# The linear score term of a graph attention layer, computed as four column groups over 128 tokens each and spread over the partitions by two transfers

## The chip, the cores and the metric

The kernel runs on one core of a Trainium2 chip. The metric is the device time of one execution in microseconds, as the median of several runs. All data are float32.

## The reference, cut to what matters

Four graph layers run over 64 graphs of 256 nodes with 128 features. Each layer takes a layer norm and a ReLU of x, applies a graph network with the shared matrix adj, and adds the result to x. The first layer is a gated network of five steps, the second a Chebyshev filter, the third a normalised convolution. The change is in the fourth, an attention layer whose pairwise scores are by far the largest piece of work:

```python
W1, W2 = (W[:, :F], W[:, F:])            # W is adj, 256 x 256; F = 128
s1 = jnp.einsum('bkf,ef->bke', x, W1)    # e runs over 256
s2 = jnp.einsum('bkf,ef->bke', x, W2)
pre = s1[:, :, None, :] + s2[:, None, :, :] + b_lin
h = jnp.where(pre >= 0, pre, ALPHA * pre)      # ALPHA = 0.2
e = jnp.einsum('bije,e->bij', h, a) + bias     # bias is adj
attn = jax.nn.softmax(e, axis=2)
out = jax.nn.sigmoid(jnp.einsum('bij,bjf->bif', attn, x))
```

The leaky rectifier is split into a clamped part, whose weighted sum over e needs one value for every (i, j, e), and a linear part. Of the linear part, what depends on i alone drops out of the softmax over j; what remains is ALPHA times the sum over e of a_e times s2_je. That is one number for each token j of each graph, the same for every row i. The kernel calls it `lin`.

## The kernel before

**Tiling.** The 64 graphs go in 32 pairs. A pair's activations are 128 x 512 tiles: features on the partitions, 2 x 256 tokens along the free dimension. A pair has two parts.

**The front** (`front(p)`) runs layers 0 to 2 of pair p and prepares layer 3: it makes `hT`, the normalised input by feature, and from it, each by one call of `project` and one eviction by ScalarE (ACT), the tiles `s2a`/`s2c` (first half of e), `lin`, `s2n`, `s1b` and `s1a`. `project` is four matmuls of 32 output columns each, which write four 32-partition strips of one PSUM bank over 512 tokens. For `lin` the stationary tile is `g2`, whose 128 columns are all the same vector, so that the bank holds the one wanted row 128 times, once on every partition. `copied` evicts it to SBUF with a 128 x 512 copy.

**The scores.** For each pair there are 128 score tiles (`NSLOT` = 32 x 64 positions, each with two halves of e, so 4096 in all). A tile `rl` is 128 x 2048: the clamped values of four rows i. It is made on VectorE (DVE) by one instruction (L652), on ACT by eight (L665), or on GpSimd (POOL) by eight (L672). TensorE (PE) reduces a tile over e with four matmuls of 32 columns over 512 (L709). Who makes a tile is not fixed: the kernel's planner decides it.

**The tail** (`tail(p, ic, ...)`) ends a block of 64 tiles: DVE adds adj to the summed scores (L558), POOL adds `lin` (L562), DVE takes the maximum (L566), ACT exponentiates (L571), PE transposes and multiplies with `h3`, ACT and POOL finish the output (L597 to L602), and the SP queue stores it (L604). There are 64 tails. `lin` is read nowhere else.

**What sets the order.** When the program is built, a list scheduler (the loop at the end of the kernel function) steps through time. Every front and tail is a generator that yields the engine of its next step and the time from which that step can run; `ran` advances an engine's planned clock by a hand-written cost, for example `PROJECT` = 0.86 for a `project` and `COPY` = 0.48 for an eviction. Whenever an engine is free by plan, the scheduler gives it a tail's step, else a front's step, else a score tile, and `in_order` then fixes the order of the engine's instructions for good. PE scores the tile that has been ready longest. At most 8, 3 and 2 tiles may be held unscored by DVE, ACT and POOL (`MOST`), and 13 buffers hold tiles. The costs therefore decide how the 4096 tiles are divided among DVE, ACT and POOL. A front may run ahead of its due time by a few steps only (`chain_ready`). Three PSUM banks are handed out by `take()` and come back through `spare`.

The SP queue issues the loads of x (`load_x(p + 1)`, when front p begins) and the stores of the tails, in the order in which the scheduler emitted them.

Of the kernel before, what the change touches and what calls it, by code (L numbers as in the profile page):

```python
# [8 lines left out]
F32 = mybir.dt.float32  # L9
# [5 lines left out]
P = 128  # L15
# [5 lines left out]
PE, DVE, ACT, POOL = ENGINES = (mybir.EngineType.PE, mybir.EngineType.DVE, mybir.EngineType.Activation, mybir.EngineType.Pool)  # L21
# [4 lines left out]
def kernel(  # L26
# [50 lines left out]
    nc = tc.nc  # L77
# [7 lines left out]
    work = ctx.enter_context(tc.tile_pool(name="work", bufs=2))  # L85
    relu_pool = ctx.enter_context(tc.tile_pool(name="relu", bufs=3))
    psum = ctx.enter_context(tc.tile_pool(name="psum", bufs=1, space=PSUM))
    banks = [psum.tile([P, NB * N], F32, name=f"bank{k}") for k in range(8)]
    s2v = banks[:2]
    s2p = banks[2].rearrange("p (b n) -> p b n", b=NB)  # L90
# [1 line left out]


    clock = dict.fromkeys((PE, DVE, ACT, POOL), 0.0)
    SEEN = {PE: 0.25, DVE: 0.14, ACT: 0.18, POOL: 0.13}
    behind = [0.0]

    def ran(engine, us, *after):
        start = max(clock[engine], 0.0, *after)
        if engine == ACT:  # L100
            behind[0] = max(0.0, behind[0] - (start - clock[ACT])) + 0.024 * us
        clock[engine] = start + us
        return clock[engine] + SEEN[engine] + (behind[0] if engine == ACT else 0.0)

    spare = [[b, 0.0] for b in banks[5:]]

    def take():

        spare.sort(key=lambda b: b[1])
        return spare.pop(0)  # L110

    def by_feature(b):
        return b.rearrange("p (b n) -> p b n", b=NB)
# [11 lines left out]
    def in_order():  # L125

        traced = nc.cur_bb.bb.instructions
        for ins in traced[done[0]:]:
            if ins.engine not in ENGINES:
                continue  # L130
            if ins.engine in last:
                tc.add_manual_dep(ins, last[ins.engine],
                                  mybir.DependencyInfo(mybir.DependencyClass.NoSync, mybir.DependencyReason.DATA),
                                  reason="program order")
            last[ins.engine] = ins.name
        done[0] = len(traced)
# [115 lines left out]
    g2 = const.tile([P, P], F32, name="g2")  # L252
# [8 lines left out]
    def side_by_side(o, w, t, start=True, stop=True):  # L261

        for g in range(0, P, 32):
            nc.tensor.matmul(o[g:g + 32], w[:, g:g + 32], t, start=start, stop=stop, skip_group_check=True)  # L264

    def flat(t):
        return t.rearrange("p b n -> p (b n)")

    def project(pp, w, t, start=True, stop=True):

        side_by_side(pp, w, flat(t), start, stop)
# [30 lines left out]
    def feat(name, **kw):  # L302
        return work.tile([P, NB, N], F32, name=name, **kw)
# [10 lines left out]
    PROJECT, MIX, TURN, PRODUCT, PRODUCTS = 0.86, 1.74, 0.69, 0.88, 2.64  # L314
    COPY, BIASED, TANH, ELEMENTS = 0.48, 0.58, 0.57, 0.61

    def norm(src, since, h):

        stats = work.tile([P, NB * NC, 6], F32, name="stats")
        mv = work.tile([P, NB * NC, 2], F32, name="mv")  # L320
        s, h = rows_of(src), rows_of(h)
        yield DVE, since
        for k in range(NB * NC):
            nc.vector.bn_stats(stats[:, k, :], s[:, k, :])  # L324
        for k in range(NB * NC):
            nc.vector.bn_aggr(mv[:, k, :], stats[:, k, :])  # L326
        nc.vector.tensor_scalar(mv[:, :, 0], mv[:, :, 0], -1.0, None, op0=OP.mult)  # L327
        t = ran(DVE, 1.12, since)
        yield POOL, t
        inverse_root(mv[:, :, 1], OP.add, LN_EPS)  # L330
        nc.gpsimd.tensor_mul(mv[:, :, 0], mv[:, :, 0], mv[:, :, 1])  # L331
        t = ran(POOL, 1.4, t)
        yield ACT, t
        for k in range(NB * NC):
            nc.scalar.activation(h[:, k, :], s[:, k, :], AF.Relu, bias=mv[:, k, 0:1], scale=mv[:, k, 1:2])  # L335
        return ran(ACT, 1.54, t)

    def copied(name, bank, t):

        c = feat(name, **(SHORT if name not in KEPT else KEPT[name]))  # L340
        nc.scalar.copy(c, by_feature(bank[0]))  # L341
        t = ran(ACT, COPY, t)
        spare.append([bank[0], t])
        return c, t

    KEPT = {"hT": dict(bufs=4), "hT3": {}, "s2n": {}, "lin": {}}

    READY = {}

    def front(p):  # L350
# [8 lines left out]
        t = yield from norm(x0, 0.0, h)  # L359
        yield PE, t, 1  # L360
        b = take()
        to_feature(b[0], h)
        t_h = t
        t = ran(PE, TURN, t, b[1])
        yield ACT, t
        hT, t_hT = copied("hT", b, t)
        for step in range(STEPS):
            yield PE, t_h, 1
            b = take()
            mix_nodes(b[0], h, adj_t)  # L370
            t = ran(PE, MIX, t_h, b[1])
# [6 lines left out]
            t = ran(PE, 2 * PROJECT, t_m, t_hT, pr[1])  # L378
# [3 lines left out]
            t = ran(ACT, TANH, t, r[1])  # L382
# [11 lines left out]
            t = ran(PE, 2 * PROJECT, t_rh, pv[1])  # L394
# [5 lines left out]
            t = ran(ACT, TANH, t)  # L400
# [4 lines left out]
            t = ran(DVE, ELEMENTS, t)  # L405
# [7 lines left out]
            hT = hT_new  # L413
            t_hT = ran(DVE, ELEMENTS)
            spare.append([pr[0], t_hT])
            yield PE, t_hT, 1
            b = take()
            to_token(b[0], hT)
            t = ran(PE, TURN, t_hT, b[1])
# [9 lines left out]
        t = ran(DVE, ELEMENTS, t)  # L429
# [6 lines left out]
        b = take()  # L436
        mix_nodes(b[0], h, adj_n)
        t = ran(PE, MIX, t_h, b[1])
# [3 lines left out]
        b = take()  # L442
        to_feature(b[0], h)
        t = ran(PE, TURN, t_h, b[1])
        yield ACT, t
        hT, t = copied("hT", b, t)
        yield PE, t_h, 1
        b = take()
        mix_nodes(b[0], h, adj_2)
        t = ran(PE, MIX, t_h, b[1])  # L450
        yield ACT, t
        c2T, t = copied("c2T", b, t)
# [3 lines left out]
        t = ran(PE, PRODUCTS, t, po[1])  # L456
# [7 lines left out]
        t = ran(DVE, ELEMENTS)  # L464
# [4 lines left out]
        t = yield from norm(x2, t, h)  # L469
        yield PE, t, 1  # L470
        b = take()
        mix_nodes(b[0], h, adj_ti)
        t = ran(PE, MIX, t, b[1])
        yield ACT, t
        yT, t = copied("yT", b, t)
# [3 lines left out]
        t = ran(PE, PRODUCT, t, po[1])  # L479
# [3 lines left out]
        t = ran(DVE, ELEMENTS, t)  # L483
# [3 lines left out]
        t = ran(ACT, COPY, t)  # L487
# [3 lines left out]
        t = ran(DVE, ELEMENTS, t)  # L491
        yield POOL, t
        inverse_root(rn, OP.max, NORM_EPS * NORM_EPS)
        t = ran(POOL, 1.25, t)
# [3 lines left out]
        for k in range(NB * NC):  # L498
            nc.vector.scalar_tensor_tensor(rows_of(x3)[:, k], pt[:, k], rn[:, k:k + 1], rows_of(x2)[:, k],
                                           op0=OP.mult, op1=OP.add)  # L500
        t = ran(DVE, 1.04, t)
# [4 lines left out]
        t = yield from norm(x3, t, h3)  # L506
        yield PE, t, 1
        b = take()
        to_feature(b[0], h3)
        t = ran(PE, TURN, t, b[1])  # L510
        yield ACT, t
        hT, t_hT = copied("hT3", b, t)
# [7 lines left out]
        t_s2c = t_s2a = ran(ACT, COPY, t_s2a)  # L520
        yield PE, t_hT, 1
        b = take()
        project(b[0], g2, hT)
        t = ran(PE, PROJECT, t_hT, b[1])
        yield ACT, t
        lin, t_lin = copied("lin", b, t)
        yield PE, t_hT, 1
        b = take()
        project(b[0], w2n[:, P:2 * P], hT)
        t = ran(PE, PROJECT, t_hT, b[1])  # L530
        yield ACT, t
        s2n, t_2 = copied("s2n", b, t)
        yield PE, t_hT, 1
        b = take()
        project(b[0], adj_t[:, 0, P:2 * P], hT)
        t = ran(PE, PROJECT, t_hT, b[1])
# [6 lines left out]
        b = take()  # L543
        project(b[0], adj_t[:, 0, 0:P], hT)
        t = ran(PE, PROJECT, t_hT, b[1])
# [6 lines left out]
                        since=(max(t_n, t_s2a, t_s2c), max(t_b, t_2)))  # L552
# [75 lines left out]
    def tile_ready(e):  # L628

        if e in begun:  # L630
            return 0.0
        n = following[half(e)]
        if n >= NSLOT or n // SLOTS not in READY or held[e] == MOST[e] or not tiles:
            return None
        return max(READY[n // SLOTS]["since"][half(e)], min(t[1] for t in tiles))
# [90 lines left out]
    def begin_front():  # L726
        p = begun_fronts[0]
        load_x(p + 1)
        begin(p, front(p))
        begun_fronts[0] += 1  # L730

    def chain_ready(key, e):

        engine, since, bank, gate = (*CHAINS[key][1], 0, None)[:4] if len(CHAINS[key][1]) < 4 else CHAINS[key][1]
        if engine != e or bank and not spare or gate and not gate():
            return None
        if not isinstance(key, tuple) and key > 0 and spare:

            due = STEPS_OF_FRONT * (scored[0] / (2 * SLOTS) - (key - 2)) / SPREAD
            if CHAINS[key][2] > due + AHEAD:  # L740
                return None
        return max(since, min(b[1] for b in spare)) if bank else since
# [7 lines left out]

    in_order()
    now = dict.fromkeys(clock, 0.0)
    for e in clock:
        clock[e] = 0.0
    while scored[0] < 2 * NSLOT or CHAINS:
# [4 lines left out]
        for key in CHAINS:  # L760
            since = chain_ready(key, e)
# [6 lines left out]
        else:  # L768
            since = tile_ready(e)
# [47 lines left out]
```

## Time and profile before

| | us |
|---|---|
| median of 3 runs | 5358.55 (5358.25 to 5358.73) |
| the profiled execution's own time | 5354.23 |
| its span | 5352.4 |
| PE busy, of the span | 5241.4 (98%) |
| DVE busy | 5221.7 (98%) |
| ACT busy | 5121.4 (96%) |
| POOL busy | 5160.9 (96%) |
| PE weight loads (PEld), overlapping PE | 1861.5 (35%) |

| `lin` and its neighbours | count | busy us | mean ns |
|---|---|---|---|
| PE matmuls `bank<-hT,g`, 128 x 512 | 256 | 34.2 | 607 |
| ACT copy of `lin`, 128 x 512 | 32 | 28.8 | 900 |
| POOL addition of `lin`, 128 x 512 | 64 | 84.3 | 1317 |

Busy time of a group is the union of its instructions' spans, and a mean is the length of one instruction's own span; instructions of one engine overlap in the profile, so what an instruction costs its engine is read from the distance between starts. The profile shows two records for every float32 matmul of the program: a `project` of four matmuls appears as eight. In the groups, L264 is the line of `side_by_side`, which serves all projections, and L341 that of `copied`.

### The profile page before, as it was taken

The page shows a single profiled execution, that of the slowest core. Times are in us where ns is not written, and L with a number is a line of the kernel's source. Part 1 is how long each engine was busy: PE and PEld are TensorE (multiplying, and loading weights), DVE is VectorE, ACT ScalarE, POOL GpSimd, SP SyncE. Part 2 cuts the span into 40 slices and gives each one's busy share as a digit, 9 for nine tenths or more (in the row PEclk, how much of TensorE's full clock was granted, in tenths as well). Part 3 has the DMA queues.
Part 4 walks back from the last instruction along what each step waited for, and adds up shares of the span by engine and source line. Part 5 has one row for each costly group of instructions (what it writes and reads, how often), then busy time and mean ns, then how long its engine had stood idle before and what let it go on. Part 6 is the DMA issues. An engine that isn't in the chain of part 4 may idle for free.

```text
span 5352.4 us, 138977 instructions
## 1 busy us (share of the span) xinstructions
PE 5241.4 (98%) x56085; PEld 1861.5 (35%) x56085; DVE 5221.7 (98%) x4322; ACT 5121.4 (96%) x13465; POOL 5160.9 (96%) x5974
## 2 busy tenths in 40 slices
PE   6999999999999999999999999999999999999998
PEld 2333333333333333333333333333333333333332
DVE  3999999999999999999999999999999999999998
ACT  3999999999999999999999999999999999999999
POOL 0999999999999999999999999999999999999999
PEclk9999999999999999999999999999999999999999
DMA  0000000000000000000000000000000000000000
GB/s 17 5 5 6 6 3 6 6 5 6 5 4 6 5 6 5 3 6 6 5 5 4 4 6 5 6 6 3 6 5 6 6 5 3 6 5 4 4 2 4
DMA packets 38839, 26.99 MB, mean 5 GB/s; under 512 B 3504, under 2 KB 38192, under 8 KB 38192
## 3 DMA queue, kind: packets, MB, share of 16 engines
q1 hardware_dynamic: 35088, 17.05, 1.1%
q8 instruction: 438, 7.18, 0.6%
q14 instruction: 209, 1.71, 0.1%
q10 hardware_dynamic: 3104, 1.05, 0.1%
HBM read 9.70 MB, written 8.39 MB: 3 GB/s over the span
## 4 chain that ended last, share of the span: by engine, by line
PE 49%; DVE 34%; POOL 9%; ACT 5%; issue 4%; DMA 0%; POOLq 0%; SPq 0%; DVEq 0%; ACTq 0%
PE bank L709 32%; DVE rl L652 28%; PE bank L264 15%; POOL rl L672 7%; ACT rl L665 3%; PE bank L292 1%; DVE d L404 1%; DVE stats L324 1%; DVE bank L408 1%; DVE hT L412 1%; DVE rh L385 1%; PE bank L285 1%; POOL sc L562 0%; DVE mv L327 0%; POOL mv L259 0%
## 5 line engine op out<-in xcount | busy, mean ns | idle before, releaser
L672 POOL TENSOR_SCALAR rl<-s2n,s1b 128x256 f32<-128x256 f32 x5328 | 4786.0, 940 | 9.7 <-ACT s1b L539 9.7
L652 DVE TENSOR_TENSOR rl<-s1a,bank 128x2048 f32<-128x2048 f32 x2015 | 4484.6, 2276 | 12.1 <-ACT s1a L548 12.1
L665 ACT ACTIVATE rl<-bank,s1b 128x256 f32<-128x256 f32 x11056 | 4392.2, 839 | 1.3
L709 PE MATMUL bank<-rl,win_n 128*32 128x512 f32 x21448 | 2654.8, 593 | 33.9 <-DVE rl L652 31.9
L709 PE MATMUL bank<-rl,win 128*32 128x512 f32 x11320 | 1487.2, 593 | 0.0
L709 PEld LDWEIGHTS bank<-rl,win_n 128*32 128x32 f32 x21448 | 678.9, 110 | 1496.4 <-issue 1214.0
L709 PEld LDWEIGHTS bank<-rl,win 128*32 128x32 f32 x11320 | 365.9, 110 | 754.4 <-issue 630.2
L264 PE MATMUL bank<-adj_t,h 128*32 128x256 f32 x5120 | 310.0, 381 | 3.8 <-ACT h L423 3.8
L264 PEld LDWEIGHTS bank<-adj_t,h 128*32 128x32 f32 x5120 | 166.6, 110 | 174.3 <-issue 58.6
L335 ACT ACTIVATE h<-x,mv 128x128 f32<-128x128 f32 x384 | 172.1, 634 | 43.3 <-POOL mv L331 42.9
L264 PE MATMUL bank<-hT,u3t 128*32 128x512 f32 x1280 | 169.5, 593 | 0.0
L264 PE MATMUL bank<-mT,w4t 128*32 128x512 f32 x1280 | 169.4, 592 | 0.0
L264 PE MATMUL bank<-mT,w 128*32 128x512 f32 x1280 | 166.8, 593 | 0.5 <-ACT bank L381 0.5
L264 PE MATMUL bank<-mT,w5t 128*32 128x512 f32 x1280 | 166.7, 592 | 0.4 <-DVE rh L385 0.4
L264 PE MATMUL bank<-rh,u5t 128*32 128x512 f32 x1280 | 166.6, 592 | 0.0
L341 ACT COPY mT<-bank 128x512 f32<-128x512 f32 x160 | 133.9, 837 | 33.1 <-PE bank L264 24.6
L396 ACT ACTIVATE bank<-bank,gate_b 128x512 f32<-128x512 f32 x160 | 141.0, 881 | 17.7 <-PE bank L264 17.7
L381 ACT ACTIVATE bank<-bank,gate_b 128x512 f32<-128x512 f32 x160 | 140.0, 875 | 15.6 <-PE bank L264 15.2
L399 ACT ACTIVATE bank<-bank,gate_b 128x512 f32<-128x512 f32 x160 | 136.3, 852 | 12.8 <-PE bank L264 12.8
L423 ACT COPY h<-bank 128x512 f32<-128x512 f32 x128 | 117.3, 916 | 29.6 <-PE bank L292 24.7
L258 POOL TENSOR_SCALAR mv<-mv 128x4 f32<-128x4 f32 x128 | 29.8, 232 | 120.1 <-DVE mv L326 112.5
L404 DVE TENSOR_TENSOR d<-bank,hT 128x512 f32<-128x512 f32 x160 | 108.4, 678 | 37.5 <-ACT bank L399 37.5
(116 smaller groups left out, 3445.0 us busy)
## 6 DMA issues: line engine op xcount, KB each, us to landing
xin<-in_x_dram SPq DMA_DIRECT2D x64, 128.0 KB, 2.3
out_dram<-o SPq DMA_DIRECT2D x64, 128.0 KB, 1.8
w_raw<-in_L_gnn_w_w_dram ACTq DMA_DIRECT2D x3, 128.0 KB, 4.3
th_raw<-in_L_gnn_Theta_dram ACTq DMA_DIRECT2D x1, 320.0 KB, 3.1
adj_n<-in_adj_dram SPq DMA_DIRECT2D x1, 256.0 KB, 4.8
w_raw<-in_L_gnn_u_w_dram ACTq DMA_DIRECT2D x2, 64.0 KB, 3.4
bias<-in_L_gnn_bias_dram ACTq DMA_DIRECT2D x2, 64.0 KB, 3.0
w<-in_L_gnn_weight_dram ACTq DMA_DIRECT2D x1, 64.0 KB, 2.8
```

The costliest lines, as they stand in the source:

```text
L264: nc.tensor.matmul(o[g:g + 32], w[:, g:g + 32], t, start=start, stop=stop, skip_group_check=True)
L335: nc.scalar.activation(h[:, k, :], s[:, k, :], AF.Relu, bias=mv[:, k, 0:1], scale=mv[:, k, 1:2])
L341: nc.scalar.copy(c, by_feature(bank[0]))
L381: nc.scalar.activation(r[0], pr[0], AF.Tanh, bias=br, scale=0.5)
L396: nc.scalar.activation(pr[0], pr[0], AF.Tanh, bias=bz, scale=0.5)
L399: nc.scalar.activation(pv[0], pv[0], AF.Tanh, bias=bh, scale=1.0)
L404: nc.vector.tensor_sub(d, by_feature(pv[0]), hT)
L423: nc.scalar.copy(h, by_token(b[0]))
L652: nc.vector.tensor_tensor(t, rows.to_broadcast(whole), ops["s2a"].unsqueeze(1).to_broadcast(whole), op=OP.min)
L665: nc.scalar.activation(t[:, g, b, :], (s2p if k else ops["s2c"])[:, b, :], AF.Relu, bias=ops["s1"][k][:, b, i:i + 1], scale=-1.0)
L672: nc.gpsimd.tensor_scalar(t[:, part, b, :], ops["s2n"][:, b, :], ops["s1"][1][:, b, i:i + 1], None, op0=OP.min)
L709: nc.tensor.matmul(pe[g * 32:(g + 1) * 32, :], w[:, k, 31 - r:63 - r], flat(t[:, g]), start=first, stop=(left[block] == 0), skip_group_che ...
```

## The change

The four matmuls that make the row now take 128 tokens each rather than all 512: strip g of the bank's partitions gets tokens 128g to 128g + 127, and every one of the 32 partitions of a strip holds the same numbers. ACT evicts the 128 x 128 result into a tile `quarter`. The SP queue then writes `quarter` to a scratch tile `row` in device memory, and a second transfer reads rows 0, 32, 64 and 96 of it back, repeated to all 128 partitions, into `lin`. `lin` has the same shape and contents as before. The planner is told of it: the matmuls are planned at 0.22, the eviction at 0.2, and each transfer, by the new helper `moved`, at 0.5 of the queue and 2.2 until it has landed. As the planned clocks differ, so does the whole order that comes after, the division of the score tiles among DVE, ACT and POOL included.

```diff
+    dram = ctx.enter_context(tc.tile_pool(name="dram", bufs=4, space=bass.MemoryType.DRAM))
...
+    queue = [0.0]
...
+    def moved(since):
+
+        queue[0] = max(queue[0], since) + 0.5
+        return queue[0] + 2.2
...
-    KEPT = {"hT": dict(bufs=4), "hT3": {}, "s2n": {}, "lin": {}}
+    KEPT = {"hT": dict(bufs=4), "hT3": {}, "s2n": {}}
...
         yield PE, t_hT, 1
         b = take()
-        project(b[0], g2, hT)
-        t = ran(PE, PROJECT, t_hT, b[1])
-        yield ACT, t
-        lin, t_lin = copied("lin", b, t)
+        for g in range(4):
+            nc.tensor.matmul(b[0][g * 32:(g + 1) * 32, 0:P], g2[:, 0:32], flat(hT)[:, g * P:(g + 1) * P],
+                             start=True, stop=True, skip_group_check=True)
+        t = ran(PE, 0.22, t_hT, b[1])
+        yield ACT, t
+        quarter = work.tile([P, P], F32, name="quarter", bufs=1)
+        nc.scalar.copy(quarter, b[0][:, 0:P])
+        t = ran(ACT, 0.2, t)
+        spare.append([b[0], t])
+        row = dram.tile([P, P], F32, name="row", bufs=2)
+        nc.sync.dma_start(row, quarter)
+        lin = feat("lin")
+        nc.sync.dma_start(flat(lin).rearrange("p (q n) -> p q n", q=4), row[0:P:32, :].unsqueeze(0).to_broadcast([P, 4, P]))
+        t_lin = moved(moved(t))
         yield PE, t_hT, 1
...
+    queue[0] = 0.0
     for e in clock:
         clock[e] = 0.0
```

## The prediction

> **What bounds the kernel now.** I read the shares of busy time first, then the table by stretches of the span (160 us each), the groups by line, the waits, and the timeline for what an instruction really costs.
>
> ```profile
> PE 5241.4 (98%) x56085; PEld 1861.5 (35%) x56085; DVE 5221.7 (98%) x4322; ACT 5121.4 (96%) x13465; POOL 5160.9 (96%) x5974
> ```
>
> No engine has room on the average. The table by stretches (columns PE, PEld, DVE, ACT, POOL busy) says where the few per cent lie:
>
> ```profile
> 0.00:160.00 160.00, 116.64 (x1205) 45.94 (x1209) 63.77 (x155) 66.06 (x134) 28.64 (x48) 0.90 0.06 16
> ...
> 2560.00:2720.00 160.00, 158.60 (x1720) 56.49 (x1716) 159.07 (x132) 155.54 (x409) 158.60 (x185) 1.00 0.02 5
> ...
> 5120.00:5280.00 160.00, 143.95 (x1259) 41.81 (x1260) 159.10 (x88) 159.94 (x443) 159.50 (x181) 1.00 0.01 3
> ```
>
> DVE has 96 of its 131 idle us in the start, where only fronts run. In the middle PE, DVE and POOL are within 1.5 us of full in 160, and ACT alone has 4.5 us free. In the last 230 us the fronts are done and PE has room, while DVE, ACT and POOL are full. So PE and the tile makers bind together for 5000 us, and the makers alone at the end. The waits agree: from 160 to 5320 us DVE waits for other engines only 10 us in all.
>
> The costliest groups, and what the change touches (count, busy us, mean ns, idle before):
>
> ```profile
> L672 POOL TENSOR_SCALAR rl<-s2n,s1b 128x256 f32<-128x256 f32 x5328 | 4786.0, 940 | 9.7 <-ACT s1b L539 9.7
> L652 DVE TENSOR_TENSOR rl<-s1a,bank 128x2048 f32<-128x2048 f32 x2015 | 4484.6, 2276 | 12.1 <-ACT s1a L548 12.1
> L665 ACT ACTIVATE rl<-bank,s1b 128x256 f32<-128x256 f32 x11056 | 4392.2, 839 | 1.3
> ...
> L264 PE MATMUL bank<-hT,g 128*32 128x512 f32 x256 | 34.2, 607 | 0.0
> ...
> L341 ACT COPY lin<-bank 128x512 f32<-128x512 f32 x32 | 28.8, 900 | 1.4 <-PE bank L264 1.4
> ```
>
> The real prices are distances between starts. In the timeline of PE, eight matmul records over 512 columns take 0.86 us; on DVE 19 tiles take 41.76, on POOL 48 instructions 42.97, on ACT eight instructions on the second half of e 2.85 and on the first half 3.19, and the 128 x 512 copy 0.48:
>
> ```profile
> 2500.11 1.04 PE L709 MATMUL bank<-rl,win 128*32 128x512 f32 x8
> 2500.97 1.04 PE L709 MATMUL bank<-rl,win_n 128*32 128x512 f32 x8
> ...
> 5208.22 3.52 ACT L665 ACTIVATE rl<-s2c,s1a 128x256 f32<-128x256 f32 x8
> 5211.41 3.25 ACT L665 ACTIVATE rl<-bank,s1b 128x256 f32<-128x256 f32 x8
> 5214.26 0.88 ACT L580 ACTIVATE wT<-bank 128x512 f32<-128x512 f32 x1
> 5214.74 7.71 ACT L665 ACTIVATE rl<-bank,s1b 128x256 f32<-128x256 f32 x20
> ```
>
> So one DVE tile costs 2.20 us, one POOL instruction 0.895 (7.2 a tile), one ACT tile 2.85 or 3.19.
>
> **What the Trainium skill says.** "Perfetto Trace Analysis", Identifying the Most-Contended Engine, warns that matmul busy time is no measure of room on TensorE because matmuls are pipelined. Here records of 1.04 us follow every 0.86, so I use 0.86; at that rate there are no gaps. "ScalarE: Activation LUTs", What ACT_TABLE_LOAD costs, prices an instruction without pointer operands at 186 ns plus 0.833 ns an element, less 93 ns of overlap: 0.52 us for 512 elements, where the trace has 0.48, and 0.20 for 128. "DMA: Bandwidth & Descriptors", Anatomy of one DMA, gives about 2 us fixed for a small transfer, stated for another issuing path; the trace shows 2.3 us to landing for the 128 KB loads of x and 1.8 for the stores.
>
> **PE.** Removed: 32 projections at 0.86 = 27.5 us. Added: 32 groups of eight records over 128 columns. The trace shows that form in `bank<-w,yT`: 32 records in 1.08 us, less the 0.27 of the last, over 31 gaps: 0.026 each, 0.21 for eight. PE sheds 0.65 x 32 = 20.8 us. Were loading of weights the limit, the chain at `th` (80 records in 2.44 us, 0.24 for eight) would be the price, and the sum 19.8.
>
> **ACT.** Each eviction falls from 0.48 to 0.20 (the page's price; two 128 x 128 outputs of L597 are 0.25 each in the trace, with a pointer operand more): 32 x 0.28 = 9.0 us, between 7.4 and 9.0.
>
> **The tiles.** These savings reach the end only as the order uses them, and the order is known before a run. I counted the instructions of both built programs. DVE makes 2009 tiles where it made 2015, POOL issues 5312 tile instructions for 5328, ACT takes 8 tiles more (312 instructions on the first half for 264, 11072 on the second for 11056). All else on these engines is equal in number. Then:
>
> - DVE: 6 x 2.20 = 13.2 us less.
> - POOL: 16 x 0.895 = 14.3 us less.
> - ACT: 48 x 0.40 + 16 x 0.356 - 9.0 = 15.9 us more.
> - PE: 20.8 us less, its 4096 tiles unchanged.
>
> **The start.** The first tile of DVE waits for `s1a` at 140.44 us, behind five projections that PE runs one after another; one is now 0.65 shorter. That is another 0.65 us off DVE and POOL. **The end** keeps its form: in both orders DVE's last tile is the fourth from last to be scored, POOL's the second from last and ACT's the last, and the closing tail is the same.
>
> **The transfers.** Per pair SP gets two issues more, 64 in all, against 128 loads and stores. The first waits for the copy, the second for the first to land, so SP stands still for some 2 us; behind it are stores and the load of a later x. A store's tile has two buffers and tails are about 81 us apart; the load of x serves a front one pair later, some 160 us. ACT's copy also waits for the first transfer of the pair before (one `quarter`), 160 us old. POOL's addition now waits for a landing. Two transfers at 2 to 5 us each end within 10 us of the copy. In the trace `lin` is copied at 2526.9 and 2691.3 us and the first block that reads it ends a full block later, near 80 us. I cost all this at nothing: at least 70 us covers it. If that cover were gone, up to 8 us would stand on POOL's queue for each of 32 pairs. The extra wait of POOL's instruction lies outside the groups shown; bounded between 0 and 0.1 us for 64 tails, at most 6 us, and I take 0. I see no reason for a gain in it.
>
> **The sum.** DVE: 13.2 + 0.65 = 13.9; POOL: 14.9; PE could give 20.8. The end is set by the makers, so the span loses 14 if their idle time stays as it is. ACT must then lose 30 us of its 231 idle (14 by the shorter span, 16 by the added work). It waits about 123 us between 160 and 5320, mostly for front steps on POOL and PE, and a shorter PE queue brings its tiles back sooner. Span 5352.4 - 14 = 5338.4. The profiled execution's own time is 1.8 more, 5340.2; the median lies 4.3 above that execution (5358.55 against 5354.23), so **5344.5**.
>
> **Rivals.**
> - *PE sets all*: if PE were the only bound, 20.8 us pass: 5337.7. For it: PE never stands still long in the middle. Against it: DVE and POOL shed only 14, and PE has room at the end. 0.13.
> - *The new order wastes it*: another plan meets other stalls. DVE has some 19 us of idle in the middle; nine more would leave 5 of the gain, 5353.5. For it: every position in the order changes, and planned times are never exact. Against it: three engines agree on the sum. 0.12, with late transfers counted here.
> - *ACT becomes the bound*: it takes eight more tiles. If its idle time in the middle is made by chains of front steps (layer norm, gates) and not by missing tiles, it does not shrink, and the others wait for ACT's tiles: 15.9 us more, 5374.5. This turns the sign once less than 16 of the needed 30 us come free. For it: 34 of its waits are `h` for POOL's norm, 30 us, untouched. Against it: the planner gives ACT a front step only when ready, and tiles otherwise. 0.05.
> - *The forecast*: 0.70, by itself 5339 to 5349.
>
> **How the numbers follow.** About 0.2%, 10.7 us, is what a measurement of this kernel can tell from no change: faster means below 5347.8. The forecast's own spread puts 0.55 of its 0.70 there; with the first rival 0.68. Within 0.2%: 0.15 from the forecast, 0.11 from the second rival: 0.26. Slower: 0.06. The range 5337 to 5354 holds the forecast, most of the first rival and half of the second.
>
> **What would show it.** Right: DVE at about 5208 us busy, POOL 5147, PE 5220, ACT 5137; the new PE group at a fourth of its cost and the copy near 0.2 us from start to start; both transfers landed within 10 us, and no wait of POOL's L579 for a DMA. Wrong: ACT's waits unchanged at about 123 us with DVE waiting for tile buffers; POOL waiting for `lin`; or DVE's idle time in the middle well above 19 us.

## The result, and the profile after

The changed kernel takes 5348.18 us (median of 16 runs) against 5358.56 for the kernel before in the same runs: 10.4 us less, a ratio of 0.9979 with a 95% interval of 0.9972 to 0.9986. In a second job (a set of runs taken together), on another chip, it took 5335.25 against 5347.41, 12.2 us less, 0.9978 (0.9969 to 0.9986). The forecast was 14 us less, 5344.5, in a range of 5337 to 5354. The prediction would call a kernel faster from 10.7 us of gain on (below 5347.8); the first job misses that by 0.4 us, the second passes it. By their intervals both gains are clear of no change.

The kernel before itself took 5347.4, 5347.7 and 5358.9 us on the three chips of the experiments, so a time is compared only with the kernel before of its own job. For the same reason the first profile of the changed kernel, an execution of 5333.93 us, is not set against the 5354.23 of the profile before: the 20 us between them are more than timed runs of the two kernels side by side show. Inside that profile counts and prices can be read. Its shares of busy time:

```profile
PE 5222.4 (98%) x56085; PEld 1864.0 (35%) x56085; DVE 5206.3 (98%) x4316; ACT 5123.7 (96%) x13529; POOL 5140.8 (96%) x5958
```

The groups of the makers and of what was changed (line, engine, shapes, count, then busy us and mean ns of one, then idle before):

```profile
L689 POOL TENSOR_SCALAR rl<-s2n,s1b 128x256 f32<-128x256 f32 x5312 | 4765.8, 928 | 9.2 <-ACT s1b L556 8.9
L669 DVE TENSOR_TENSOR rl<-s1a,bank 128x2048 f32<-128x2048 f32 x2009 | 4469.3, 2276 | 11.2 <-ACT s1a L565 11.2
L682 ACT ACTIVATE rl<-bank,s1b 128x256 f32<-128x256 f32 x11072 | 4410.4, 913 | 1.0
...
L536 ACT COPY quarter<-bank 128x128 f32<-128x128 f32 x32 | 20.6, 645 | 0.0
L531 PE MATMUL bank<-hT,g 128*32 128x128 f32 x256 | 13.3, 277 | 0.0
```

DVE makes six tiles fewer, POOL issues 16 instructions fewer and ACT more, as counted. The PE group of the row fell from 34.2 to 13.3 us, 20.9 less where 20.8 were worked out; from start to start a group fell from 0.86 to 0.22 us. For the copy one must not read the mean of 645 ns, because instructions of one engine overlap in the profile; the timeline of ACT shows that the next instruction starts 0.14 us after it:

```profile
2679.96 0.82 ACT L536 COPY quarter<-bank 128x128 f32<-128x128 f32 x1
2680.10 2.14 ACT L682 ACTIVATE rl<-bank,s1b 128x256 f32<-128x256 f32 x4
```

In the same profile's list of DMA issues (size of one, median us to landing) the transfers stand so, and in the waits of the SP queue as the third line:

```profile
lin<-row SPq DMA_DIRECT2D x32, 256.0 KB, 7.6
...
row<-quarter SPq DMA_DIRECT2D x32, 64.0 KB, 1.5
```

```profile
SPq L542 <- DMA row<-quarter: 44.0, 32, 3.3
```

SP stands 44 us in all before the second transfers, 1.4 us each. No wait of POOL for a DMA is listed, and `lin`'s addition (L579) waited only 2.8 us, once, for DVE.

### The profile page after: what moved, and what is told of

Its sections match the earlier page's. It is cut to its first block, busy times and chain, and to the rows that moved or that the text cites. A ratio compares the mean times of both kernels' runs of the same rounds, so it can differ in the third digit from the quotient of the medians.

```text
span 5332.2 us, 139121 instructions
## 1 busy us (share of the span) xinstructions
PE 5222.4 (98%) x56085; PEld 1864.0 (35%) x56085; DVE 5206.3 (98%) x4316; ACT 5123.7 (96%) x13529; POOL 5140.8 (96%) x5958
## 4 chain that ended last, share of the span: by engine, by line
DVE 52%; PE 27%; POOL 12%; issue 6%; ACT 2%; DMA 0%; DVEq 0%; POOLq 0%; SPq 0%; ACTq 0%
DVE rl L669 43%; PE bank L726 17%; POOL rl L689 11%; PE bank L271 9%; ACT rl L682 2%; DVE bank L415 1%; DVE hT L419 1%; DVE d L411 1%; DVE stats L331 1%; DVE rh L392 1%; PE bank L299 1%; DVE mv L334 1%; DVE nmx L583 1%; DVE mv L333 0%; POOL mv L266 0%
## 5 line engine op out<-in xcount | busy, mean ns | idle before, releaser
L689 POOL TENSOR_SCALAR rl<-s2n,s1b 128x256 f32<-128x256 f32 x5312 | 4765.8, 928 | 9.2 <-ACT s1b L556 8.9
L726 PE MATMUL bank<-rl,win 128*32 128x512 f32 x11384 | 1503.3, 593 | 0.0
L348 ACT COPY mT<-bank 128x512 f32<-128x512 f32 x160 | 147.6, 922 | 37.1 <-PE bank L271 28.0
L388 ACT ACTIVATE bank<-bank,gate_b 128x512 f32<-128x512 f32 x160 | 152.4, 953 | 14.8 <-PE bank L271 14.4
L403 ACT ACTIVATE bank<-bank,gate_b 128x512 f32<-128x512 f32 x160 | 147.8, 924 | 13.3 <-PE bank L271 13.2
L406 ACT ACTIVATE bank<-bank,gate_b 128x512 f32<-128x512 f32 x160 | 148.9, 930 | 11.2 <-PE bank L271 11.0
L430 ACT COPY h<-bank 128x512 f32<-128x512 f32 x128 | 132.2, 1032 | 23.3 <-PE bank L299 23.2
L682 ACT ACTIVATE rl<-s2c,s1a 128x256 f32<-128x256 f32 x312 | 149.3, 902 | 0.0
```

Of the source, the lines that this page charges most:

```text
L388: nc.scalar.activation(r[0], pr[0], AF.Tanh, bias=br, scale=0.5)
L403: nc.scalar.activation(pr[0], pr[0], AF.Tanh, bias=bz, scale=0.5)
L406: nc.scalar.activation(pv[0], pv[0], AF.Tanh, bias=bh, scale=1.0)
L430: nc.scalar.copy(h, by_token(b[0]))
L682: nc.scalar.activation(t[:, g, b, :], (s2p if k else ops["s2c"])[:, b, :], AF.Relu, bias=ops["s1"][k][:, b, i:i + 1], scale=-1.0)
L689: nc.gpsimd.tensor_scalar(t[:, part, b, :], ops["s2n"][:, b, :], ops["s1"][1][:, b, i:i + 1], None, op0=OP.min)
```

## The experiments

All have the timed runs of the kernel before beside them on the same chip. With the kernel before, the first three make a table of two by two, operations against order; the fourth leaves out the transfers. Where an expectation names an absolute time, it was counted from the 5358.6 us of the kernel before in the first job. These four ran on a chip where that kernel takes 5347.41, so only differences are compared.

**The changed kernel again.**

> The changed kernel once more. In its first profile the span fell by 20.2 us, while its timed executions fell by only 10.4. If that profile shows what the change does, timed executions and profile should agree here on some 14 to 20 us less. If the profile was one lucky execution, the new profile lies near 5346 and the timed median again near 5348.

5335.25 against 5347.41, profile 5335.78: profile and timed runs agree on this chip, and the gain is 12.2 us, not 20. Neither branch came true as stated: the gain is a little under 14, and the kernel is not back near 5348. The first profile is like this one in time and also in the pace of POOL, whose 5312 tile instructions are busy 4765.8 us there and 4765.9 here. On the chip where the kernel before takes 5358.9, POOL is slower (last section). On which chip the first profile was taken is not on record.

**The changed operations in the old order.**

```diff
-        t = ran(PE, 0.22, t_hT, b[1])
+        t = ran(PE, PROJECT, t_hT, b[1])
...
-        t = ran(ACT, 0.2, t)
+        t = ran(ACT, COPY, t)
...
-        t_lin = moved(moved(t))
+        t_lin = t
```

> The changed operations in the order of the kernel before: the planner is told the old costs (0.86, 0.48, no transfer), so DVE keeps 2015 tiles and POOL its 5328 instructions. If the gain reaches the end through the division of tiles alone, as predicted: only the start is shorter and stalls behind PE shrink a little, 0.5 to 4 us less than before, 5354 to 5358. If PE sets all: 20.8 us less, 5338.

5346.56 against 5347.41: 0.85 us less, ratio 0.9999 (0.9990 to 1.0007). In the trace the instructions of DVE, ACT and POOL follow one another as in the kernel before, one for one but for the form of the copy. PE and ACT have less to do, and nothing that is clear of noise comes of it.

**The old operations in the new order.** In the kernel before:

```diff
-        t = ran(PE, PROJECT, t_hT, b[1])
+        t = ran(PE, 0.22, t_hT, b[1])
...
-        lin, t_lin = copied("lin", b, t)
+        lin = feat("lin")
+        nc.scalar.copy(lin, by_feature(b[0]))
+        t = ran(ACT, 0.2, t)
+        spare.append([b[0], t])
+        t_lin = moved(moved(t))
```

> The operations of the kernel before in the order of the changed kernel: four matmuls over 512 tokens, a 128 x 512 copy, no transfer, but the planner is told 0.22 and 0.2. DVE has 2009 tiles, ACT 1423. If the order alone brings the gain, near 5348. If PE really has to be relieved for it, as predicted, PE and ACT run 20.8 and 9 us behind the plan, and the time is that of before or worse: 5356 to 5368.

5336.54 against 5347.41: 10.9 us less, ratio 0.9980 (0.9972 to 0.9988). My expectation failed: I had expected the time of before or worse if PE must be relieved. A kernel that computes exactly what the kernel before does, with the same instructions but for their order and the makers of some tiles, has nearly the whole gain; the changed kernel is 1.3 us below it, which the intervals do not separate.

**Without the transfers.**

```diff
-        row = dram.tile([P, P], F32, name="row", bufs=2)
-        nc.sync.dma_start(row, quarter)
-        lin = feat("lin")
-        nc.sync.dma_start(flat(lin).rearrange("p (q n) -> p q n", q=4), row[0:P:32, :].unsqueeze(0).to_broadcast([P, 4, P]))
+        lin = lin_0
```

> The changed kernel without its two transfers: lin is one constant tile of zeros, so the linear term is left out of the scores. The order on PE, ACT, DVE and POOL is that of the changed kernel. If the transfers cost nothing, as predicted: within 1 us of the changed kernel, 5347 to 5349. If they take the missing part of the gain in timed executions: 5336 to 5340.

5334.70, beside 5335.25 with them: 0.5 us, which the intervals do not separate from nothing.

What the order does is read from the stretch of 160 to 5300 us, in profiles of one chip (us, then PE, PEld, DVE, ACT, POOL busy). The new operations in the old order, then the changed kernel, then the old operations in the new order:

```profile
160.00:5300.00 5140.00, 5074.77 (x54600) 1801.86 (x54596) 5123.96 (x4152) 5006.00 (x13250) 5091.02 (x5890) 1.00 0.03 7
```

```profile
160.00:5300.00 5140.00, 5084.27 (x54688) 1810.09 (x54684) 5125.35 (x4151) 5038.81 (x13350) 5089.00 (x5885) 1.00 0.03 7
```

```profile
160.00:5300.00 5140.00, 5097.24 (x54687) 1812.31 (x54679) 5125.78 (x4152) 5047.02 (x13348) 5088.54 (x5885) 1.00 0.02 5
```

The stretch is of equal length but not of equal work: in the new order a kernel is 10 to 11 us further on at its end. DVE and POOL are equally full in all three. ACT's idle time is 134, 101 and 93 us: in the new order it does tiles in time that it stood idle in the old one, whether or not PE has been relieved (the longer copies alone fill 32 x 0.32 = 10 us, which covers the step from 101 to 93). PE's is 65, 56 and 43 us, of which 15 to 18 fall after 5120 us, where PE has room in every order. So with the old matmuls in the new order 28 us are left to it in the 4960 us before that: little, but enough.

My theory now was: the time follows the tiles that DVE and POOL give up, for ACT has idle time to take them; which operations the kernel has matters little. The rival: PE binds, and an order that plans it too fast stalls. The next eight were made on the planner's numbers.

**Which of the two costs moved the tiles.** The old operations, with one cost told at a time (0.22 for the matmuls, the true 0.48 for the copy; then 0.86 and 0.2).

> The operations of the kernel before; the planner is told 0.22 for the four matmuls of the linear term, and the true 0.48 for its copy. The order gives DVE 2011 tiles, ACT 1420, POOL 665. Theory (the time follows the tiles that DVE and POOL give up, as ACT has idle time to take them): DVE sheds 4 x 2.2 = 8.8, POOL 8 x 0.9 = 7.2, so 6 to 9 us less than before. Rival (the copy's planned cost carries it): no difference, within 2 us.

> The operations of the kernel before; the planner is told 0.2 for the copy of the linear term, and the true 0.86 for its matmuls. The order gives DVE 2014 tiles, ACT 1417, POOL 665. Theory: DVE sheds 2.2, POOL 7.2, so 1 to 4 us less than before. Rival (the copy's planned cost carries it): 8 to 11 us less.

The first took 5352.00, the second 5356.19, against 5358.86: 6.9 us less, 0.9987 (0.9981 to 0.9994), and 2.7 less, 0.9994 (0.9986 to 1.0002), the latter not clear of no change. Both lie where the tiles put them; the planned cost of the matmuls carries the larger part. Told together with the planned landing of the transfers, the two costs move six tiles off DVE, told singly four and one; what moves the last one was not tried.

**Planning the scoring faster than it is.** The changed kernel with the cost of a tile's scoring lowered in `score`; the 4096 tiles multiply it.

```diff
-        free = ran(PE, PROJECT, since, t_pe.get(block - 2, 0.0))
+        free = ran(PE, 0.80, since, t_pe.get(block - 2, 0.0))
```

> The changed kernel with one number of the planner changed: the scoring of a tile is planned at 0.80 of TensorE, which really takes 0.86. The order gives DVE 2001 tiles, ACT 1433, POOL 662 (2009, 1423, 664 in the changed kernel). Theory: DVE sheds another 8 x 2.2 = 17.6, POOL 16 x 0.9 = 14.4, which leaves some 13 to 17 us less than the changed kernel, 25 to 29 less than before. Rival (TensorE binds, so an order that plans it too fast stalls there): no faster than the changed kernel, or slower.

> The same with 0.70 for the scoring of a tile. DVE 1995 tiles, ACT 1442, POOL 659. Theory: DVE sheds 14 x 2.2 = 30.8 against the changed kernel, POOL 40 x 0.9 = 36; ACT takes 19 tiles more, some 55 us, of which it has about 100 idle; 25 to 31 us less than the changed kernel, 37 to 43 less than before. Rival (TensorE binds): with some 55 us of idle time left in TensorE, stalls eat the gain and the time is at or above that of the changed kernel.

5422.25 and 5511.37 against 5358.86: 63 us more, 1.0118 (1.0104 to 1.0131), and 153 more, 1.0284 (1.0270 to 1.0298). The theory fell in this form. The tiles went to ACT as counted, and the time rose. The waits of DVE at 0.80 say how (us in total, times, longest):

```profile
DVE sc L575 <- PE bank L726: 52.0, 34, 5.0
DVE rl L669 <- ACT s1a L565: 23.6, 3, 12.0
DVE bank L489 <- PE bank L271: 16.0, 11, 7.4
```

In the changed kernel on its second chip the first line of these is only the closing tail:

```profile
DVE sc L575 <- PE bank L726: 5.7, 1, 5.7
```

The plan puts a tail's first step into DVE's order where it believes the block is scored. PE is not there yet, and DVE, whose order is fixed, holds back the tiles behind it. But PE is not simply full there: it also waits more for the tiles that DVE holds back. Between 160 and 5300 us, in the changed kernel and then at 0.80:

```profile
PE bank L726 <- DVE rl L669: 30.8, 53, 1.7
```

```profile
PE bank L726 <- DVE rl L669: 83.7, 120, 3.1
```

PE's idle time in that stretch rises from 56 to 107 us. So an order that asks more of PE than it has loses time, and the loss is in stalls of both engines on each other rather than in PE's own work. How the 63 us divide among these stalls was not worked out.

I refined the theory: the plan may be wrong on PE by about the idle time that PE has, some 55 us over the run, and within that the tiles decide.

> The changed kernel; the scoring of a tile is planned at 0.855 of TensorE instead of 0.86, 20.5 us in all 4096. DVE 2006 tiles, ACT 1427, POOL 663 (2009, 1423, 664 in the changed kernel). Theory (tiles given up by DVE and POOL count, as long as the plan is wrong on TensorE by no more than its idle time of some 55 us): DVE 6.6, POOL 7.2 less, so 4 to 7 us less than the changed kernel, 15 to 19 less than before. Rival (any optimism on scoring stalls the makers): at or above the changed kernel.

> The same at 0.84: 82 us too little in all, more than the idle time of TensorE. DVE 2008 tiles, ACT 1425, POOL 663. By tiles alone 2 to 7 us less than the changed kernel. Theory: the plan runs ahead of TensorE by more than its idle time, so some stalls show, and the time is that of the changed kernel or up to 25 us more (0.80, wrong by 246 us, measured about 75 more). Rival (only the reordering at random decides): anywhere.

> The changed kernel; one more projection of the front, that of s2n, is planned at 0.22 although it takes 0.86: 20.5 us too little, in 32 places. DVE 2009 tiles, ACT 1423, POOL 664, as in the changed kernel. Theory (tiles count): within 3 us of the changed kernel. Rival (room on TensorE in the plan counts by itself): 7 to 11 us less.

> The operations of the kernel before, with its true costs but for the scoring, planned at 0.855. DVE 2012 tiles, ACT 1418, POOL 666 (2015, 1415, 666 before). Theory: DVE sheds 6.6, POOL nothing, so 0 to 5 us less than before. Rival (optimism on scoring stalls the makers): more than before.

In one job, against 5347.71 for the kernel before:

| kernel | planned too little on PE | tiles DVE / ACT / POOL | us | ratio |
|---|---|---|---|---|
| changed, scoring at 0.855 | 20 us | 2006 / 1427 / 663 | 5329.54 | 0.9967 (0.9955 to 0.9979) |
| changed, s2n's projection at 0.22 | 20 us | 2009 / 1423 / 664 | 5336.37 | 0.9979 (0.9972 to 0.9987) |
| changed, scoring at 0.84 | 82 us | 2008 / 1425 / 663 | 5352.36 | 1.0010 (1.0003 to 1.0016) |
| before, scoring at 0.855 | 20 us | 2012 / 1418 / 666 | 5345.72 | 0.9998 (0.9990 to 1.0006) |

Four of four lie in the range that was expected of them, if the changed kernel, which was not in this job, is put at its 12.2 us of gain from the second job; the range of the third was wide (up to 25 us above it). The same 20 us bring 6.8 us where they move tiles (first row, every run of it below every run of the second) and nothing where they don't (second row, 11.3 us less than before, within 1 us of the changed kernel's 12.2). At 82 us a small shift of tiles (one off DVE, one off POOL) is eaten: DVE then waits 19.6 us for PE at L575, 21 times:

```profile
DVE sc L575 <- PE bank L726: 19.6, 21, 2.7
```

The first row beats both kernels: 18.2 us less than before. Where between 20 and 82 us the turn lies was not measured, so "about PE's idle time" is an estimate that fits these points.

One thing was read off afterwards. Wherever the plan is wrong on PE by 20 us or less, the gain is near the smaller of what DVE and POOL shed, at 2.20 us a tile and 0.895 an instruction. With only the matmuls' cost told it is 6.9 where POOL sheds 7.2, with only the copy's 2.7 where DVE sheds 2.2. The old operations in the new order gain 10.9 where DVE sheds 13.2, the first row of the table 18.2 where DVE sheds 19.8, and the last row 2.0 where POOL sheds nothing. This fits makers that bind together; as a rule it was not put to a run of its own, and the two smallest gains are not clear of no change.

## Why the prediction held, point by point

**The prices and counts** held. PE's saving was worked out at 20.8 and is 20.9; ACT's copy costs 0.14 from start to start rather than the 0.20 taken, and 0.465 before rather than 0.48, so ACT sheds some 10 us, a little above the 7.4 to 9.0 given; the tiles are those of the built order. DVE's busy time is 5206 (5208 forecast), PE's 5222 (5220), POOL's 5141 (5147), ACT's 5124 (5137). Part of ACT's difference is the chip: its tile instructions follow one another every 356.8 ns there and every 357.5 in the profile before, some 8 us over 11 000.

**The sum** was 14 and measured 10.4 and 12.2. On the second chip it can be split, by DVE's timeline in the changed operations with the old order and in the changed kernel (start and length of each, in us). First the old order:

```profile
140.68 2.29 DVE L669 TENSOR_TENSOR rl<-s1a,bank 128x2048 f32<-128x2048 f32 x1 [11.93 <-ACT s1a L565]
...
5319.49 8.89 DVE L669 TENSOR_TENSOR rl<-s1a,bank 128x2048 f32<-128x2048 f32 x4
5333.01 0.69 DVE L575 TENSOR_TENSOR sc<-bank,adj_n 128x512 f32<-128x512 f32 x1 [4.62 <-PE bank L726]
```

Then the changed kernel:

```profile
140.36 2.29 DVE L669 TENSOR_TENSOR rl<-s1a,bank 128x2048 f32<-128x2048 f32 x1 [11.90 <-ACT s1a L565]
...
5307.39 8.89 DVE L669 TENSOR_TENSOR rl<-s1a,bank 128x2048 f32<-128x2048 f32 x4
5321.99 0.69 DVE L575 TENSOR_TENSOR sc<-bank,adj_n 128x512 f32<-128x512 f32 x1 [5.72 <-PE bank L726]
```

From first tile to last batch the new order takes 11.8 us less, where six tiles at 2.20 are 13.2: the makers shed the time "if their idle time stays as it is", and this was 1.4 too good. From the last batch to the first step of the closing tail (5333.01 and 5321.99) it is 1.1 longer: "the end keeps its form" is true of the sequence of tiles and not of its times. With the 0.3 by which the first tile is earlier, these make the 11.0 us between the two spans (5345.0 and 5334.0). The start differs by 0.3 between these two, both of which have the short projection; the old operations in the new order start at 141.0, 0.6 later than the changed kernel, which agrees with the 0.65 of the prediction but does not show it, since profiles with the same matmuls differ by as much (140.36 here and 138.57 in the first profile of the same kernel).

**The reason** was in part wrong, and the right total hid it. The step that failed is "PE and the tile makers bind together" with its companion that ACT's idle time shrinks because "a shorter PE queue brings its tiles back sooner". ACT's idle time did shrink, from 134 to 101 us in the stretch above, but it is just as small, 93, with PE's queue as long as before. And PE relieved of its 20.8 us in the old order brought 0.85 us, not clear of noise, while the old operations in the new order brought 10.9. PE, though idle for only 28 to 47 us between 160 and 5120 us, did not bind. What the change did was to make the planner believe in 20 us more room on PE and 9 on ACT, so that it gave ACT eight more tiles. That the total came out near all the same is because I took the division of tiles from the built order and let the makers, not PE, set the end. The sum also needed ACT's idle time to shrink; that it did, and not for the reason I gave, was luck.

**The rivals.** *PE sets all* was wrong at 20.8 us: relieving PE in the old order brought 0.85. *ACT becomes the bound* did not happen; the sign can turn, but by another road: an order that plans PE too fast by 82 us loses 4.7 against before. *The new order wastes it* was true by some 2.5 us, the 1.4 and 1.1 above.

**The transfers at nothing** were right: leaving all 64 of them out moved the median by 0.5 us. The second takes 7.6 us to land, more than the 2 to 5 taken, but with the first 9.1 in all by the medians, within the 10 that were allowed and far inside the 70 us of cover. The Trainium skill, "DMA: Bandwidth & Descriptors", Anatomy of one DMA, fits about 2.0 us fixed plus the bytes over 436 GB/s, for another issuing path. As an estimate from that page this gives 2.2 us for the first transfer, where 1.5 were measured, and 2.6 for the second, where 7.6 were: it does not carry over to the second.

## What to carry to other kernels

Where a list scheduler with hand-written costs lays out the work, an edit acts twice, through the machine and through the plan, and the two are told apart by building the cross: new operations with the old costs, old operations with the new costs. Here nearly all of the gain came through the plan, from planned costs alone. Before an operation is made cheaper to relieve a full engine, try what the plan does if it is only told so; and keep the untruth small: here 20 us in all, less than PE's idle time, did no harm, and 82 us, more than it, cost all that had been gained, because an engine whose order is fixed waits where the plan put a step too early.

## What was not expected of the hardware

Reading four rows of 512 bytes repeatedly, to fill 128 partitions with 256 KB, lands in 7.6 us (6.2 to 8.3); the load of `adj_n`, as large and of distinct data, lands in 4.5 to 5.4 in all profiles. Why was not tried.

Three chips ran the same unchanged kernel in 5347.4, 5347.7 and 5358.9 us, a spread as large as the effect under study. The traces show two engines at another pace. First the new operations in the old order, on the chip of 5347.4, then the old operations with the copy planned at 0.2, on that of 5358.9:

```profile
L689 POOL TENSOR_SCALAR rl<-s2n,s1b 128x256 f32<-128x256 f32 x5328 | 4778.1, 923 | 9.5 <-ACT s1b L556 9.5
```

```profile
L683 POOL TENSOR_SCALAR rl<-s2n,s1b 128x256 f32<-128x256 f32 x5320 | 4786.6, 933 | 9.8 <-ACT s1b L550 9.6
```

Eight instructions fewer are busy 8.5 us longer. In the traces, from start to start, POOL's tile instructions take 895.5 ns on the two faster chips and 898.0 on the slow one, some 13 us over the run, and ACT's on the second half of e 356.8 and 357.5, some 8 us; DVE's tiles (2.197 us) and PE's scoring (0.859) are alike. That the kernel takes 11 us more for it fits makers that set the end; why the paces differ is not shown. Nor is the level quite fixed to the chip's number on record: the first execution of the kernel before is 5347.25 on the slow chip and 5357.89 on the one of 5347.7, all others there being at the chip's own level.
